# Layer 1's query and key rows by seven Strassen block products, with the weight sums made as layer 1 begins

## The chip, the cores and the metric

The kernel runs on one core of one Trainium2 chip, as one launch. The metric is the device time of one execution in microseconds (us). Below, PE is TensorE, ACT is ScalarE, DVE is VectorE, POOL is GpSimd, and SP is the engine whose queue issues most of the DMAs. b is a batch (0 to 7). KB are KB per partition.

## The reference

Two layers work on x of 8 batches, 512 channels and 1024 tokens, all in FP32. Layer 0 is group norm, eight-head attention over all tokens, a projection and a residual. Layer 1, cut to what matters here:

```python
importance = sum over channels of x*x               # one number per token
idx = top_k(importance, 256)                        # the selected tokens of a batch
q_sel, k_sel, v_sel = (Wq x)[idx], (Wk x)[idx], (Wv x)[idx]
q_sel, k_sel = layer_norm(q_sel), layer_norm(k_sel)
attended = softmax(clip(q_sel k_sel^T * scale)) v_sel
out = Wv x, with the selected tokens' rows replaced by attended
return x + Wo out
```

The changed product is that of the 256 selected tokens (512 channels each) with Wq and Wk side by side: a 256 x 512 matrix times a 512 x 1024 matrix, once per batch.

## The kernel before, in words

**Order.** Layer 0 and layer 1 each lie in a region in which every engine issues its instructions in the order in which the code emits them (L721 and L1518). Between the two regions the scheduler may merge an engine's instructions, so layer 1's first ones can run in the tail of layer 0 where what they need is free. Layer 1's order is written out by hand in two lists, `BATCH` (L63 on) and `END`. A word is a step, its number the part, and each `-` or `+` puts the batch one back or one ahead. `layer1` (L700) walks `BATCH` once per batch t from -1 to 5, and then `END` for the last two batches and what is left of batch 5. In a turn t, `row3` is batch t, `selt0-` batch t-1 and `back2--` batch t-2. Batch 0's rows, counts and values are made in layer 0, so the first turn that does full work is t = 1: batch 1's rows and values beside batch 0's selection.

**A batch in layer 1.** PE transposes eight blocks of 128 tokens (`row`, L277); ACT squares them with a sum (`square`) and keeps them for a DMA out (`keep`, `put`). `spread` and `imp` lay the importance out as a row, and DVE counts for each token how many rank before it (`count`, L317: two compares with a sum and one masked by the lower triangle `before`). `place`, `pick`, `holder` and `who` turn counts into indices; POOL gathers the selected rows (`getx`), PE turns them (`selt`) and ACT keeps them (`selk`, the tile `selT`). `qk` (L516) makes the four blocks of 128 rows: q and k, each of two row blocks, each by four matmuls of 128x512 into one PSUM bank. `stats`, `root` and `norm` (L525 to L549) are the layer norm on those banks, DVE but for the square root on ACT; `normt`, `scale` and `score` make the scores, `clip` to `probk` the softmax, `att`, `attk` and `attput` the attended rows. POOL fetches them back into the values (`fetch`), PE turns the values (`back`), DVE adds the residual (`add`), and SP stores. The values themselves, for the tokens in blocks i and i+4, are seven Strassen products in the steps `va` to `vf` (L404) on sums of token blocks that POOL makes (`xs`, L387, eight adds of 128x128) and sums of weights that POOL makes once (`combine_vo`, L369, four of 128x512, into the tile tvo).

**Memory.** The pools of layer 0 that are released before layer 1 lie one behind the other, by the sizes of their tiles: w0 (8.6 KB), mix (3 KB), op0 with the attention outputs o (24 KB), ep with the 14 score buffers e (56 KB), and then mp0, ap, rp0 and sp. Layer 0's last steps use free e buffers for the last residual tiles (xr_last) and the first counts. Layer 1's pools start at the same byte: rp (12.3 KB), up with two value tiles V (32 KB), mp (47 KB) and op with the residual tiles y (six of 2 KB). All tiles of a pool wait for every user of the released pools on whose bytes the pool lies. tvo and the token sums lie elsewhere, in a pool that both layers share.

**The turn from layer 0 to layer 1.** Layer 0's `finish` (L1506) runs the last output projections (PE L899) and adds their residual on DVE (L1127); each xr_last goes out by an SP DMA (L1130). PE's first instruction of layer 1 waits for the last of those DVE adds.

Of the kernel before, what the change touches and what calls it, by code (L numbers as in the profile page):

```python
# [11 lines left out]
F32 = mybir.dt.float32  # L12
# [53 lines left out]
back6--- row3 square1 xs1 back4--- keep2 square3 back7--- va1 inv-- put2 va0 keep3 put4 row0  # L66
keep1 add6--- ka1 add7--- ka0 put1 put3 att0-- xs0 vb1 vb0 kb0 vc0 row6 square0 kb1 add4---
square6 holder- vd0 who- add3--- kc0 keep6 row7 keep0 row5 square5 kg0 vd1 att1-- keep5 square7
getx- keep7 ve0 finite kf1 kc1 attk1-- kf0 va2 attk0-- xs2 attput-- fetch7-- kd0 fetch4--
spread0 imp0 vc1 fetch3-- ka2 spread1 va3 selt0- imp1 selk0- count1 fetch6-- count7 selt1-  # L70
selk1- fetch2-- vb2 kg1 vf1 fetch5-- vput1- count4 kf2 qk1- ke1 count0 ve1 qk0- qk2- xs3 ka3
put0 stats1- vb3 kd1 root1- back5-- norm1- stats0- kb2 put7 vput2- vput4- fetch1-- count3 vput5-
add5-- stats2- root0- qk3- norm0- vd2 vput7- vput0- stats3- root2- kc2 fetch0-- back1-- kb3
root3- vf0 normt0- vput6- ke0 norm2- vd3 back2-- back0-- normt1- vput3- put5 add1-- scale0-
scale1- vc2 vf2 norm3- normt2- count6 ke2 getv- vc3 normt3- add2-- kc3 kg2 add0-- scale2- kg3
scale3- score0- count2 score1- put6 row4+ square4+ ve3 clip- row1+ row2+ keep4+ ve2 exp0- kd3
vf3 kd2 kf3 probt- count5 place back3-- pick1 square2+ pick0 ke3 probk-
"""
END = """
square1- inv--- row7- keep2- back6---- put4- row6- put2- keep1- square7- xs3- row3- row0-  # L80
att1--- put1- keep7- put7- square3- holder-- add3---- row5- attk1--- va3- keep3- square5- row0
keep5- square0- who-- square6- put5- back7---- back4---- vput2-- add7---- finite- add6----
att0--- keep6- spread0- spread1- getx-- add4---- ka3- imp0- row7 keep0- row1 selt0-- imp1- row4
selk0-- square7 selt1-- kf3- put3- put0- selk1-- keep7 count4- count3- vput7-- square4 square1
put7 keep4 xs2- qk0-- count0- attk0--- stats0-- qk1-- count6- va2- stats1-- keep1 attput---
put6- fetch5--- count5- ka2- root1-- kf2- square0 norm1-- keep0 vput4-- qk2-- vb3- vb2- put1
fetch1--- stats2-- put0 row2 kb2- row6 count2- put4 root2-- square2 vd2- square6 row3 kb3- qk3--
fetch7--- square3 keep2 fetch2--- norm2-- fetch6--- count1- kc2- vf2- root0-- vc2- norm0-- row5
vput6-- ke2- square5 kg2- keep3 normt0-- vd3- keep5 kc3- stats3-- root3-- vput1-- vc3- count7-
va0- ve2- scale0-- fetch0--- vput5-- fetch4--- finite norm3-- normt1-- fetch3--- spread1 kd2-  # L90
ka0- put5 imp1 normt3-- normt2-- xs0- scale3-- spread0 kg3- place- pick1- vf3- scale1-- va1-
keep6 pick0- imp0 back7--- holder- scale2-- score1-- score0-- count5 vb0- back6--- who- ve3-
count3 clip-- kb0- vd0- back0--- ka1- getx- back3--- ke3- vput3-- add6--- kf0- vput0-- xs1- vb1-
add7--- back2--- add3--- kc0- put6 selt0- vf0- vc0- exp0-- add2--- kd3- count6 inv-- selt1-
selk0- vput3- count4 selk1- qk1- probt-- probk-- put2 count7 qk2- kg0- getv-- att0-- attk0--
count1 count2 count0 kb1- place att1-- put3 pick1 ve0- vd1- ke0- pick0 attk1-- stats1- qk0- kd0-
holder vc1- stats0- attput-- who back1--- back5--- kc1- kg1- vf1- root1- ve1- ke1- getx add1---
qk3- vput4- stats2- kd1- va2 kf1- add5--- vput0- norm1- selt0 root0- vput6- fetch2-- norm0-
selk0 back4--- add4--- selt1 ka2 selk1 vput5- normt0- stats3- fetch4-- fetch3-- root2- norm2-
qk2 vput1- stats2 normt1- qk0 root3- kf2 vput2- fetch1-- fetch0-- norm3- qk1 va3 root2 xs3  # L100
scale1- xs2 scale0- normt3- norm2 stats1 stats0 scale3- root1 normt2- scale2- ka3 qk3 vb2 kb2
score0- add0--- vput7- root0 score1- stats3 norm0 root3 vd2 norm3 getv- back4-- clip- exp0-
normt2 back0-- scale2 norm1 vb3 vsel1 inv- probt- add4-- kf3 normt0 add0-- normt3 probk- normt1
fetch7-- scale1 scale3 att0- attk0- kc2 back6-- vselk1 att1- vc2 kg2 vc3 fetch5-- scale0 attk1-
fetch6-- attput- score0 fetch2- kb3 add6-- vd3 fetch1- fetch0- va1 score1 fetch4- clip vsel0
back3-- back5-- ka1 vselk0 fetch6- kc3 kg3 exp0 ve2 fetch5- xs0 back1-- vf2 fetch7- add3-- probt
add1-- fetch3- va0 kd2 ke2 back2-- probk ka0 inv att0 att1 attk0 ve3 attk1 back7-- vb0 xs1 kb0
vb1 add5-- add2-- attput kb1 kf1 vc0 vd0 fetch2 back4- vd1 add7-- kc0 kc1 kf0 vf0 kg0 vc1 add4-
fetch6 kd3 ve0 back6- fetch3 kg1 ve1 kd0 ke0 back3- back1- add6- fetch4 fetch0 kd1 fetch1 vf1
vf3 ke1 fetch5 back5- back2- back7- back0- back4 add3- back6 add1- add2- add5- back2 add0- back0  # L110
ke3 fetch7 add7- add4 add6 back5 add2 back1 back7 add0 back3 add5 add7 add3 add1
# [35 lines left out]
def attention_then_topk_attention(  # L147
# [61 lines left out]
    before = const.tile([P, P], F32, tag="before", name="before")  # L209
# [107 lines left out]
    def count(b, j):  # L317

        cnt = get("r1", ("count", b), [P, 3, NB], "count", 2)
        imps = tiles["imp", b]  # L320
        mine = tiles["col", b][:, j : j + 1]
        lo, hi = j * P, (j + 1) * P
        junk = tiles.get("junk")
        if junk is None:
            junk = pools["rp"].tile([P, N], F32, tag="junk", name=f"junk_{b}_{j}", bufs=1)
        if lo:
            nc.vector.tensor_scalar(
                junk[:, :lo], imps[:, :lo], mine, None, ALU.is_ge, ALU.add,
                accum_out=cnt[:, 0, j : j + 1],
            )  # L330
        else:
            nc.vector.memset(cnt[:, 0, 0:1], 0.0)
        nc.vector.tensor_scalar(
            junk[:, lo:], imps[:, lo:], mine, None, ALU.is_gt, ALU.add,
            accum_out=cnt[:, 1, j : j + 1],
        )
        nc.vector.scalar_tensor_tensor(
            junk[:, lo:hi], imps[:, lo:hi], mine, before, ALU.is_equal, ALU.mult,
            accum_out=cnt[:, 2, j : j + 1],
        )  # L340
# [28 lines left out]
    def combine_vo():  # L369
        b11, b12, b21, b22 = (  # L370
            w["vo"][:, 2 * k : 2 * k + 2, part] for k in range(2) for part in (LEFT, RIGHT)
        )
        t = vp.tile([P, NB, 2 * P], F32, tag="v", name="tvo").rearrange(
            "p (n k) c -> p n k c", k=2
        )
        t1, t2, t3, t4 = (t[:, i] for i in range(4))
        for out_, x_, op_, y_ in (
            (t3, b22, ALU.subtract, b12), (t2, t3, ALU.add, b11),
            (t4, b21, ALU.subtract, t2), (t1, b12, ALU.subtract, b11),
        ):  # L380
            nc.gpsimd.tensor_tensor(out_, x_, y_, op_)
        w["products"] = {1: b11, 2: b21, 3: b22, 4: t4, 5: t1, 6: t2, 7: t3}
# [21 lines left out]
    def value_product(n, bank_, first, at=0):  # L404
        def step(b, i):
            out_ = bank((bank_, b, i))[:, at : at + SPAN]
            for k in range(2):
                if n in (1, 2, 4):
                    left = token_block(b, k + 2 * (n != 1), i + NB // 2 * (n == 4))
                else:  # L410
                    left = tiles["xs", b, i][:, {5: 0, 6: 1, 7: 2, 3: 3}[n], k]
                nc.tensor.matmul(  # L412
                    out_, left, w["products"][n][:, k], start=(first and k == 0),
                    stop=(k == 1), skip_group_check=True,
                )
# [100 lines left out]
    def qk(b, i):  # L516
        which, rb = divmod(i, RT)
        pp = bank(("pp", b, i))
        for k in range(CT):
            nc.tensor.matmul(  # L520
                pp, tiles["selT", b][:, k, ts(rb, P)], w["qk"[which]][:, k, :],
                start=(k == 0), stop=(k == CT - 1),
            )

    def stats(b, i):  # L525
        bs = pools["mp"].tile([P, 6], F32, tag="bs", name=f"lbs_{b}_{i}", bufs=4)
        nc.vector.bn_stats(bs, tiles["pp", b, i])
# [11 lines left out]
    def normal(b, i):  # L539
# [8 lines left out]
        rows_ = get("mp", ("rows", b, which), [P, RT, C], "rows", 2)  # L548
        nc.vector.tensor_scalar(  # L549
            rows_[:, rb, :], tiles["pp", b, i], tiles["mv", b, i][:, 0:1], t,  # L550
            ALU.subtract, ALU.mult,
        )
        done("pp", b, i)
# [33 lines left out]
    def clip(b, _):  # L587

        psc = tiles["sc", b].rearrange("p (a n) -> p a n", n=TOP)
        fin = pools["mp"].tile([P, RT, TOP], F32, tag="sfin", name=f"sfin_{b}", bufs=1)  # L590
# [64 lines left out]
    def residual(b, i):  # L655
        ct, hf = divmod(i, NH)
        t = get("op", ("y", b, i), [P, HALF], "y", 6)
# [11 lines left out]
    def add(b, i):  # L669
# [19 lines left out]
        "vsel": vsel, "vselk": vselk, "selt": selt, "selk": selk, "qk": qk, "stats": stats, "root": root,  # L689
# [10 lines left out]
    def layer1():  # L700
        with ExitStack() as st:
# [19 lines left out]
            with tc.manual_schedule(engines=ORDERED):  # L721
                combine_vo()
# [916 lines left out]
```

## Time and profile before

| | us |
|---|---|
| three runs | 2358.97, 2359.34, 2359.86 |
| median | 2359.34 |
| the profiled execution, own time | 2355.33 |
| its span | 2353.0 |
| PE busy | 2317.2 (98%) |
| DVE busy | 1875.6 (80%) |
| ACT busy | 1479.1 (63%) |
| POOL busy | 1432.8 (61%) |

Layer 1 fills the span from 1909.87 us, PE's first instruction of it, to the end. A row of the view by stretches gives the stretch, its length, the busy time of PE, PE's weight loads, DVE, ACT and POOL with their instruction counts, the granted PE clock (1.00 is full), the DMA share and GB/s. A row of the timeline gives start, length, engine, line, operation, what it writes and reads, and in brackets the idle time before it with the instruction that ended it. In the chain of waits a row is start, length and what ran. An FP32 matmul of the code is two instructions in the trace, a transpose one.

### The profile page before, as it was taken

What the parts mean: (1) busy time and instruction counts of PE and PEld (TensorE: products, weight loads), DVE (VectorE), ACT (ScalarE), POOL (GpSimd) and SP (SyncE); (2) the same over time, 40 slices, a digit from 0 to 9 for tenths busy, and PEclk for the clock granted to TensorE, in tenths of its full rate; (3) what the DMA queues carried; (4) which work ended last, traced back from release to release, by engine and by line L of the source; (5) the groups of instructions that cost most, each with busy time, mean ns of one, the idle gap of its engine ahead of it and who ended that gap; (6) DMA issues with size and microseconds to landing.
All of it is one profiled execution on the core that took longest, in us unless ns stands there. A gap on an engine that the chain in (4) does not pass through costs nothing.

```text
span 2353.0 us, 36692 instructions
## 1 busy us (share of the span) xinstructions
PE 2317.2 (98%) x13164; PEld 1053.6 (45%) x13164; DVE 1875.6 (80%) x3020; ACT 1479.1 (63%) x2024; POOL 1432.8 (61%) x890
## 2 busy tenths in 40 slices
PE   7999999999999999999999999999999999999998
PEld 3333443344344334433443344334433357777766
DVE  4889988988898888888988898888787456777774
ACT  3678766776777577757776777677666534444632
POOL 2668655866676677657765776676556724444334
PEclk9999999999999999999999999999999999999999
DMA  5112222322231222222322222222323443666655
GB/s 197 48 44 67 75 76 70 102 69 73 79 96 53 82 82 89 59 79 79 91 69 77 89 82 60 84 68 55 102 82 117 139 170 118 224 217 226 225 171 173
DMA packets 201236, 244.41 MB, mean 104 GB/s; under 512 B 41930, under 2 KB 111306, under 8 KB 201056
## 3 DMA queue, kind: packets, MB, share of 16 engines
q1 hardware_dynamic: 175392, 198.51, 26.5%
q10 hardware_dynamic: 18144, 31.48, 3.7%
q0 software_dynamic: 7520, 12.09, 1.9%
q8 instruction: 104, 1.70, 0.3%
q14 instruction: 76, 0.62, 0.1%
HBM read 181.42 MB, written 73.14 MB: 108 GB/s over the span
## 4 chain that ended last, share of the span: by engine, by line
PE 89%; DVE 4%; DMA 2%; ACT 2%; issue 2%; POOL 1%; SPq 0%; ACTq 0%; DVEq 0%; POOLq 0%
PE sc L1278 19%; PE av L1358 17%; PE g L1034 15%; PE g L899 10%; PE g L1076 7%; PE b_px L412 4%; PE b_pp L520 4%; DVE high L1292 2%; PE b_py L412 1%; PE den L1374 1%; PE b_sc L582 1%; PE first L899 1%; PE b_pa L629 1%; DVE e L1339 1%; PE last L899 1%
## 5 line engine op out<-in xcount | busy, mean ns | idle before, releaser
L1347 POOL TENSOR_TENSOR es<-es,e 128x1024 f32<-128x1024 f32 x384 | 911.1, 2373 | 167.7 <-ACT e L1342 149.8
L1339 DVE TENSOR_TENSOR e<-e,ns 128x1024 f32<-128x1024 f32 x512 | 611.3, 1205 | 7.3 <-ACT ns L1335 7.3
L1286 ACT COPY e<-sc 128x1024 f32<-128x1024 f32 x512 | 501.7, 1016 | 170.2 <-DVE high L1292 101.7
L1342 ACT ACTIVATE e<-e 128x1024 f32<-128x1024 f32 x512 | 533.3, 1063 | 91.4 <-DVE e L1339 83.9
L1292 DVE TENSOR_TENSOR high<-sc,high 128x1024 f32<-128x1024 f32 x384 | 469.4, 1222 | 121.3 <-PE sc L1278 95.9
L1278 PE MATMUL sc<-q,k 64*128 64x512 f32 x2048 | 512.3, 617 | 4.1 <-DVE high L1292 2.5
L1358 PE MATMUL av<-e,v 128*64 128x512 f32 x2048 | 489.8, 598 | 0.6 <-ACT e L1342 0.5
L1347 POOL TENSOR_TENSOR es<-e,e 128x1024 f32<-128x1024 f32 x64 | 152.5, 2382 | 435.8 <-ACT e L1342 435.8
L1278 PEld LDWEIGHTS sc<-q,k 64*128 64x128 f32 x2048 | 174.5, 186 | 269.9 <-issue 146.9
L1358 PEld LDWEIGHTS av<-e,v 128*64 128x64 f32 x2048 | 135.8, 137 | 292.5 <-issue 235.2
L1034 PE MATMUL g<-wqkv,mix_qk 128*64 128x512 f32 x960 | 231.0, 602 | 1.3 <-POOL wqkv L944 1.3
L899 PE MATMUL g<-o,wp 128*64 128x512 f32 x912 | 206.8, 596 | 0.0
L1034 PE MATMUL g<-x,mix_qk 128*64 128x512 f32 x720 | 169.8, 593 | 0.2 <-ACT v L1093 0.2
L1034 PEld LDWEIGHTS g<-wqkv,mix_qk 128*64 128x64 f32 x960 | 60.9, 136 | 155.2 <-issue 115.7
L899 PEld LDWEIGHTS g<-o,wp 128*64 128x64 f32 x912 | 63.0, 137 | 135.4 <-issue 132.9
L520 PE MATMUL b_pp<-w,selT 128*128 128x512 f32 x256 | 114.0, 593 | 0.0
L1292 DVE TENSOR_TENSOR high<-sc,e 128x1024 f32<-128x1024 f32 x64 | 77.6, 1213 | 38.0 <-ACT e L1286 37.6
L1034 PEld LDWEIGHTS g<-x,mix_qk 128*64 128x64 f32 x720 | 51.6, 137 | 103.3 <-issue 89.7
L648 POOL DMA_INDIRECT V<-sa,at x64 | 64.6, 1009 | 54.1 <-issue 15.2
L426 ACT COPY V<-b_px 128x256 f32<-128x256 f32 x112 | 39.7, 374 | 88.4 <-PE b_px L412 81.2
L1410 POOL TENSOR_TENSOR o<-o,ri 128x512 f32<-128x512 f32 x64 | 81.8, 1278 | 20.8 <-ACT o L1405 10.5
L1303 DVE STREAM_TRANSPOSE mT<-high 128x512 f32<-128x512 f32 x128 | 90.3, 705 | 1.7
(228 smaller groups left out, 2811.1 us busy)
## 6 DMA issues: line engine op xcount, KB each, us to landing
nb<-negd SPq DMA_DIRECT2D x128, 256.0 KB, 3.7
x<-in_x_dram SPq DMA_DIRECT2D x32, 512.0 KB
ri<-rid SPq DMA_DIRECT2D x128, 128.0 KB, 2.9
sx<-xT ACTq DMA_DIRECT2D x64, 256.0 KB, 2.4
mix_qk<-mixd SPq DMA_DIRECT2D x120, 128.0 KB, 2.5
xr<-in_x_dram SPq DMA_DIRECT2D x58, 256.0 KB, 3.3
x1d<-xr SPq DMA_DIRECT2D x58, 256.0 KB, 2.4
sv<-V ACTq DMA_DIRECT2D x56, 256.0 KB, 2.4
```

The source lines that it names most:

```text
L412: nc.tensor.matmul(out_, left, w["products"][n][:, k], start=(first and k == 0), stop=(k == 1), skip_group_check=True,)
L520: nc.tensor.matmul(pp, tiles["selT", b][:, k, ts(rb, P)], w["qk"[which]][:, k, :], start=(k == 0), stop=(k == CT - 1),)
L899: nc.tensor.matmul(out[r, :], wide_[:, r], moving, start=(k == 0), stop=(k == CT - 1),)
L1034: nc.tensor.matmul(pt[r, :], weights[:, k, r], moving[:, k, :], start=(first and k == 0), stop=(k == 1), skip_group_check=True,)
L1076: nc.tensor.matmul(pt[ts(r, HD), ts(j, P)], tokens[:, k, j * P + r * HD : j * P + r * HD + HD], weights[:, k, :], start=(first and j + k = ...
L1278: nc.tensor.matmul(sc[:, hh, :], ks[p][r, ts(j, P)], qs[p][r, ts(hf, HALF)], start=True, stop=True,)
L1286: nc.scalar.copy(raw[t, j], banks["s", t, j])
L1292: nc.vector.tensor_tensor(high[t], banks["s", t, j], raw[t, 0] if j == 1 else high[t], ALU.max)
L1339: nc.vector.tensor_tensor(raw[t, j], raw[t, j], high[t], ALU.add)
L1342: nc.scalar.activation(raw[t, j], raw[t, j], AF.Exp, scale=QK_SCALE)
L1347: nc.gpsimd.tensor_add(sums[t], raw[t, 0] if j == 1 else sums[t], raw[t, j])
L1358: nc.tensor.matmul(avs[t][HD * hh : HD * hh + HD, :], vs[p // 2][:, j, (p % 2) * P + HD * hh : (p % 2) * P + HD * hh + HD], e[:, hh, :], s ...
```

## The change

1. `qk` is replaced by seven products (steps `qa` to `qg`), each two matmuls of 128x512 per half of the channels: a Strassen form with two row blocks, two halves of the channels, and q and k as the two column blocks. Sums of the selected rows (`qs`) are four POOL adds of 128x256, written into a half of the token-sum tile. Products share three banks: qx gets 1, 6, 7 and 4 one on top of the other, qy 5 and 3, qz 2.
2. Between products a bank's state is taken: `ra`, `rb` and `rc` are ACT copies of 128x512, `rf`, `rg` and `rd` are DVE adds of a bank to the SBUF tile `rows`. `stats` and `norm` read three of the four row blocks from `rows` in SBUF, and one from the bank.
3. The sums of Wq and Wk (`combine_outputs`, four POOL adds of 128x1024, one of them in place) follow those of Wv Wo at the start of layer 1's region. Their tile of 12 KB is the first of the pool up.
4. The mask `before` and the unused output `junk` of the counts are BF16.
5. For room, a temporary of `clip` shares the slot of `sT`, and there are five y tiles, not six. rp is 10.3 KB, up 44 KB, mp 45 KB, and op starts 8 KB further on.
6. `BATCH` and `END` are new lists.

```diff
-    before = const.tile([P, P], F32, tag="before", name="before")
+    before = const.tile([P, P], BF16, tag="before", name="before")
...
+    def combine_outputs(name, blocks, in_place):
+        b11, b12, b21, b22 = blocks
+        if in_place:
+            t = pools["up"].tile([P, 3, 2, C], F32, tag=f"t{name}", name=f"t_{name}")
...
+        t2, t3, t4 = (t[:, i] for i in range(3))
+        t1 = b12 if in_place else t[:, 3]
         for out_, x_, op_, y_ in (
             (t3, b22, ALU.subtract, b12), (t2, t3, ALU.add, b11),
             (t4, b21, ALU.subtract, t2), (t1, b12, ALU.subtract, b11),
         ):
             nc.gpsimd.tensor_tensor(out_, x_, y_, op_)
+        w[name, "products"] = {1: b11, 2: b21, 3: b22, 4: t4, 5: t1, 6: t2, 7: t3}
+
+    def combine_weights1():
+        combine_outputs("vo", [
+            w["vo"][:, 2 * k : 2 * k + 2, part] for k in range(2) for part in (LEFT, RIGHT)
+        ], False)
+        combine_outputs("qk", [
+            w[name][:, 2 * k : 2 * k + 2, :] for k in range(2) for name in "qk"
+        ], True)
...
-    def qk(b, i):
+    def selected_sums(b, _):
+        t = tiles["ss", b] = tiles["xs"][:, int(b != B - 2)]
+        a11, a12, a21, a22 = (
+            tiles["selT", b][:, 2 * q : 2 * q + 2, ts(rb, P)] for rb in range(RT) for q in range(2)
+        )
+        s1, s2, s3, s4 = (t[:, n] for n in range(4))
...
+    def selected_product(n, bank_, first):
+        def step(b, _):
+            out_ = bank((bank_, b))
+            for k in range(2):
+                if n in (1, 2, 4):
+                    left = tiles["selT", b][:, k + 2 * (n != 1), ts(int(n == 4), P)]
+                else:
+                    left = tiles["ss", b][:, {5: 0, 6: 1, 7: 2, 3: 3}[n], k]
+                nc.tensor.matmul(
+                    out_, left, w["qk", "products"][n][:, k], start=(first and k == 0),
+                    stop=(k == 1), skip_group_check=True,
+                )
...
+    def selected_take(which, rb, add_of=None):
+        def step(b, _):
+            out_ = rows_of(b, which)[:, rb, :]
+            if add_of is None:
+                nc.scalar.copy(out_, bank(("qx", b)))
+            else:
+                nc.vector.tensor_tensor(out_, bank((add_of, b)), out_, ALU.add)
...
+        "qs": selected_sums, "qa": selected_product(1, "qx", True),
+        "qb": selected_product(6, "qx", False), "qc": selected_product(5, "qy", True),
+        "qd": selected_product(7, "qx", False), "qe": selected_product(3, "qy", False),
+        "qf": selected_product(4, "qx", False), "qg": selected_product(2, "qz", True),
+        "ra": selected_take(0, 0), "rb": selected_take(1, 0), "rc": selected_take(1, 1),
+        "rd": selected_take(1, 0, "qy"), "rf": selected_take(0, 0, "qz"),
+        "rg": selected_take(1, 1, "qy"), "stats": stats, "root": root,
...
-                combine_vo()
+                combine_weights1()
```

The new `BATCH`, whole, in which the prediction follows steps:

```
put4 row3 square1 square3 va0 inv-- keep2 back7--- back4--- keep1 keep3 put1 put3 add7---
back6--- xs0 add3--- put2 att1-- att0-- va1 ka0 vb0 attk0-- kb0 attk1-- row5 attput-- holder-
ka1 row7 vd0 square5 xs1 row0 add6--- who- kc0 square0 row6 kf1 vc0 getx- square7 kg0 square6
keep7 vb1 keep0 keep5 ve0 put0 xs2 finite vput6- spread0 kb1 imp0 spread1 add4--- vc1 kf0 vd1
va2 row4+ imp1 kc1 keep6 count7 selt0- fetch4-- kg1 selk0- count5 fetch3-- ve1 vput2- fetch1--
ka2 square4+ selt1- fetch2-- count3 selk1- fetch6-- qa- qs- keep4+ qg- vput5- ra- vput1-
fetch0-- vput0- va3 qb- rb- kd1 vb2 fetch5-- qd- vput4- kb2 rf- stats0- ka3 root0- count2
fetch7-- count6 rc- qc- kd0 kf3 rg- qf- put5 norm0- stats1- stats3- qe- back2-- vf0 back5-- xs3
root1- vd2 rd- kc2 put7 back1-- put6 vf1 add2-- stats2- vc3 vf2 norm1- add1-- root3- root2-
normt0- ke0 normt1- ke1 vb3 back0-- vput3- norm3- scale1- norm2- add0-- count0 scale0- vc2
normt2- normt3- vput7- kb3 getv- scale2- kg2 scale3- vd3 ke2 kc3 score0- score1- row2+ count1
add5-- ve2 kg3 clip- back3-- row1+ vf3 kd2 kf2 ve3 exp0- kd3 count4 probt- place pick0 square2+
probk- ke3 pick1
```

In the old list the token sums `xs1` stood fourth, and `xs0` behind `att0--`; `vb1` and `vb0` were the first steps to read them.

## The prediction

> **What bounds the kernel now.** I read the page's first part (PE busy for 98% of the span), then the view by stretches for layer 1, then the chain of waits, then the timelines of the turn between the layers. Two stretches in the middle of layer 1:
>
> ```profile
> 2000.00:2050.00 50.00, 49.83 (x265) 38.88 (x264) 35.39 (x112) 26.54 (x64) 23.32 (x40) 1.00 0.69 231
> 2050.00:2100.00 50.00, 49.84 (x268) 39.12 (x267) 33.13 (x103) 24.68 (x62) 20.73 (x36) 1.00 0.69 230
> ```
>
> PE is busy for 49.8 of 50 us; DVE, next, for 33 to 35. The chain runs through PE, and its `qk` rows return at a fixed distance:
>
> ```profile
> 2042.79 3.43 PE b_pp L520 x8
> 2047.08 6.87 PE b_pp L520 x16
> ...
> 2099.55 3.43 PE b_pp L520 x8
> ```
>
> The first and last rows are `qk1-` of two batches: 56.76 us a batch. Eight instructions take 3.43 us, so one 512-column instruction is 0.429 us of PE's time. The other steps by the same chain: a value product of 256 columns 0.86, `va` 1.73, a turn of one block 0.44. PE's work in the old list, so summed, is 56.4 us a batch; only some 0.4 us of a batch is waiting. So in layer 1 the time is PE's work, plus what PE waits at its beginning and end.
>
> **What PE saves.** Before, 16 matmuls or 32 instructions a batch; after, 7 products of 2 matmuls, 28 instructions. Four fewer, 4 x 0.429 = 1.72 us a batch, eight batches: **-13.7 us**. As PE is full from turn 1 to the last `back`, all of it is on the path if the rest keeps up.
>
> **What the products add on other engines, per batch.** ACT: three copies of 128x512, 0.59 us each (the row of `keep`): 1.8 us on 25 busy in 50. DVE: three adds of 128x512 from PSUM, 0.68 each (the row of `add`): 2.0. Off again: three `norm` passes that no longer read PSUM, 0.81 each before; a 128x1024 pass in SBUF takes 0.81 too (the one norm pass of layer 0 on DVE), so at most half, 1.2 us. DVE gains 1 us on some 39 in a batch. POOL: four adds of 128x256, between 0.46 (128x128) and 1.28 (128x512), say 0.75: 3 us on 25. None becomes the bound; I cost them at nothing, with PE as cover. The BF16 mask and `junk`: rows 0.36 (masked) and 1.28 us (1024 wide), all FP32; between no change and halved, on DVE, which is not on the path: nothing, at most 7 us a batch less on DVE. Fewer y slots and the shared slot of `clip`: the next user comes many microseconds later (`clip` 44 us behind the `att` that frees `sT` in the new `BATCH`): nothing.
>
> **New waits between the products.** A product may not add to a bank before the former state is taken. In the new list qb stands two steps of PE (`qg` 1.72, `va3` 1.73) behind qa, for a copy of 0.59. Between qb and qd there is only `vb2`, 0.86, for `rb`, 0.59: 0.27 spare. Between qd and qf there is `qc`, 1.72, for `rc`, 0.59, but `rc` queues on ACT behind `root0`, with a table load 1.28 and 0.2. `root0` waits for `rf` (0.68) and `stats0` (0.70 + 0.18 + 0.15) on DVE, which may start when qg ends, 6.0 us before qd's end (`va3`, qb, `vb2`, qd). Needed before qf: 0.68 + 1.03 + 1.48 + 0.59 = 3.8 us of a 6.0 + 1.7 = 7.7 us way, so DVE or ACT may be 3.9 us late. `qe` waits for `rg`: 1.72 (qf) for 0.68. POOL's sums stand behind five `fetch` at 1.3 us each, which can begin some 9 us before qb: they fit. Bounds: from -3 (the new lists close the 0.4 us a batch that PE waits now) to +8 us (1 us in each batch). I take **+0.5**.
>
> **The weight sums.** This is the dear part. POOL's own rows for such adds, and its first sums of tokens in layer 1:
>
> ```profile
> 1795.24 7.24 POOL L1347 TENSOR_TENSOR es<-es,e 128x1024 f32<-128x1024 f32 x3
> ...
> 1820.91 1.27 POOL L381 TENSOR_TENSOR tvo<-w 128x512 f32<-128x512 f32 x1 [2.95 <-ACT w L1223]
> 1822.26 1.28 POOL L381 TENSOR_TENSOR tvo<-tvo,w 128x512 f32<-128x512 f32 x1
> ```
>
> ```profile
> 1871.59 0.46 POOL L402 TENSOR_TENSOR xs<-x_q,x_k 128x128 f32<-128x128 f32 x1
> ```
>
> The sums for Wv Wo ran at 1820.9, in a gap of layer 0, because their tile is free then. The first eight token sums followed at 1871.6, 44 us before PE read them. The new four adds have 1024 elements; three such adds take 7.24 us above, so four take 9.6. POOL keeps its order in layer 1's region, so **the token sums of batch 1 come behind them**. And their tile is in the pool up, 10.3 to 54.3 KB from where layer 0's pools begin: on mix, on the attention outputs o (11.6 to 35.6) and on ep (from 35.6). All tiles of a pool wait for every user of those, and ep's last user is the DMA out of xr_last. That such waits are real shows in SP's waits, chain and timeline:
>
> ```profile
> SPq L658 <- DMA x1d<-xr_last: 2.0, 1, 2.0
> ```
>
> ```profile
> 1909.85 2.43 DMA x1d<-xr_last
> ```
>
> ```profile
> 1912.35 1.75 SPq L658 DMA_DIRECT2D y<-x1d  x4
> ```
>
> The y pool touches only the last 0.4 KB of ep, and its first load still waited until that DMA landed, at 1912.28. So the new adds start at 1912.35, not in layer 0's tail. They end at 1912.35 + 9.6 = 1921.95. `xs0` follows: by the row 1871.59 and those behind it, its second and sixth add (the ones that `vb0` reads) end 1.0 and 2.8 us after its start, so at 1924.7. PE before:
>
> ```profile
> 1914.27 1.03 PE L412 MATMUL b_px<-w,x_q 128*128 128x256 f32 x4
> ...
> 1915.57 1.96 PE L412 MATMUL b_px<-tvo,xs 128*128 128x256 f32 x8
> ```
>
> Four `row` and two `va` (1909.87 to 1915.13) come ahead, in the new list too, and then `vb0`. There PE now waits until 1924.7: `vb0` would have ended at 1916.0 and ends at 1925.1, **+9.1 us**. POOL, not PE, sets the end of this stretch; `getx` of batch 0 comes behind `xs1`, at about 1929.1, and lands before PE reaches `selt0` (some 13 us of PE's steps later). PE's own waits of this stretch, 1.1 us for `col` and 0.7 for a value add, go mostly, as the others catch up: **-1.5**.
>
> **The clock.** The trace shows what an idle PE costs afterwards. PE waited 1.89 us for POOL in layer 0's tail:
>
> ```profile
> 1847.16 0.64 PE L1374 MATMUL den<-es,ones 128*32 128x256 f32 x8 [1.89 <-POOL es L1347]
> 1847.72 5.40 PE L345 MATMUL g<-w,x 128*128 128x512 f32 x8
> ```
>
> Eight matmuls that take 3.43 us took 5.40; by stretches of 1 us the granted clock (the third column from the end) was
>
> ```profile
> 1848.00:1849.00 1.00, 1.00 (x3) 0.25 (x3) 1.00 (x2) 0.88 (x3) 0.00 (x0) 0.68 0.50 180
> 1849.00:1850.00 1.00, 1.00 (x3) 0.48 (x2) 1.00 (x2) 1.00 (x2) 0.00 (x0) 0.50 0.28 94
> 1850.00:1851.00 1.00, 1.00 (x3) 0.48 (x2) 1.00 (x2) 0.93 (x1) 0.00 (x0) 0.50 0.02 8
> 1851.00:1852.00 1.00, 1.00 (x2) 0.35 (x2) 1.00 (x2) 0.00 (x0) 0.94 (x1) 0.61 0.07 4
> ```
>
> about 3.4 us at half (1.00 again from 1852), 1.7 us lost. After the 11.5 us without work at the kernel's start it lasted longer:
>
> ```profile
> 13.36 6.39 PE L1147 MATMUL bias_row<-wp,bqkv 128*128 128x512 f32 x8
> ```
>
> 6.39 us for 3.43: 3.0 lost. A wait of 9 us lies between: **+2.4**.
>
> The Trainium skill ("TensorE: Matmul & The Clock Gate", "What's actually happening") speaks against such a gap: it says the clock halves after at least one idle window of about 3.4 us and comes back after at least one busy one. The wait of 1.89 us above was already enough, so the measured rows decide; by the page alone the loss would be 1.7 us or more.
>
> **Sum.** -13.7 + 0.5 + 9.1 - 1.5 + 2.4 = -3.2 us. On the profiled execution's 2355.33 that is 2352.1; the median of the runs is 4.0 higher, so 2359.34 - 3.2 = **2356.1**. The end itself I leave as it is: PE's work behind the last `att` (17.8 us before, 18.6 after, by the lists) runs beside eight fetches at 1.3 us, whose landing ends the kernel.
>
> **Rivals.**
> *The weight sums run early* (in layer 0's tail, as the old ones did). For it: POOL is busy for only 33 of 50 us at 1800 to 1850. Against it: the place of the tile. The wait, the clock and the credit go: -13.7 + 0.5 = -13.2, but 9.6 us more on POOL ahead of the sums es that PE already waited 1.89 us for costs 0 to 4. About 2347.
> *The bank hand-over becomes PE's wait* (slower than before). Place: `rc` behind `root0`, each batch. It decides once DVE or ACT are more than 3.9 us late there; two counts (1.85 us each: 1024 elements in two compares and a mask) run just ahead. Each microsecond beyond costs eight. At 1.2 us: 2356.1 - 0.5 + 9.6 = 2365. Against it: DVE idles 15 of 50 us.
> *The lists also close old waits* or PE finds the clock sooner: -3.5 - 0.7 on the sum, about 2352.
>
> **How the numbers follow.** Chances: my sum 0.68 (by its bounds 2353 to 2360), early sums 0.15, hand-over 0.10, better lists 0.07. Within 0.2% (about what a measurement of this kernel can tell from no change) is 2354.6 to 2364.1. Faster: early sums 0.15, better lists 0.06, a quarter of my sum 0.17: 0.38. Slower: 0.08 of the hand-over and 0.02 of mine: 0.10. Same: 0.52. Range 2347 to 2361.5: it leaves out half of the early sums, nearly all of the hand-over and 0.03 of my sum, below 2 in 10.
>
> **What would show it.** Right: the first POOL adds of 128x1024 in layer 1 start at about 1912 and end near 1922; PE idle some 9 us from 1915, released by POOL's token sums; granted clock 0.5 for 3 to 6 us behind it; 28 instructions of 128x512 a batch, and batches 55.0 us apart. Wrong: those adds before 1900; or PE waits for ACT or DVE ahead of qb, qd, qf or qe; or batches over 56 us apart.

## The result, and the profile after

The changed kernel is slower: 2361.86 us in the median of 22 runs (2358.97 to 2365.89), and 2356.31 for the kernel before in the same rounds (22 runs, 2353.84 to 2360.07). The ratio is 1.0026, 95% interval 1.0020 to 1.0032. In a second set of rounds it was 1.0011 (1.0002 to 1.0020). I had forecast 0.9986. The changed kernel's median came out the same both times (2361.86 and 2361.36 us); that of the kernel before lay between 2354.6 and 2360.0 on five occasions, so where a few microseconds matter I lean below on the traces, each of which is one execution.

The span is 2359.8 us (own time 2361.53). Layer 0 ended 1.9 us earlier than in the trace of before, which is not the change's doing: in four of the fourteen traces, that of before among them, PE runs at half clock for 3.4 us behind its wait of 1.9 us at 1847, and their layer 1 begins at 1909.7 to 1910.4; in the ten others it begins at 1907.1 to 1908.5. From PE's first row of layer 1 to the end it is **451.8 us against 443.1**; I had predicted -3.2, and it is +8.7. First the middle, a stretch of 50 us:

```profile
2050.00:2100.00 50.00, 49.84 (x257) 38.01 (x256) 36.15 (x109) 24.59 (x62) 25.03 (x44) 1.00 0.69 232
```

PE is as full as before. DVE is busy for 40.6 us a batch over three whole batches, and for 39.6 before: the 1 us more that I had put down. The chain of waits gives the distance of the batches, by the first product of two batches, one batch apart:

```profile
2048.03 1.72 PE b_qx L550 x4
...
2103.11 1.72 PE b_qx L550 x4
```

55.08 us; from the first to the fourth such row 55.0 on average, and 56.76 before. That is the saving as predicted. The loss is at both ends of layer 1. The view of PE's waits in layer 1:

```profile
PE b_px L424 <- POOL xs L414: 11.5, 2, 10.9
PE b_pt L282 <- ACT xT L292: 2.7, 1, 2.7
...
PE b_py L424 <- DVE V L442: 1.5, 1, 1.5
```

The columns are the total, the number of waits and the longest. The first row was predicted at 9.1, the other two were not. The timelines of POOL and PE show the first:

```profile
1913.88 2.34 POOL L385 TENSOR_TENSOR t_qk<-w 128x1024 f32<-128x1024 f32 x1 [24.48 <-DMA sx<-xT]
...
1923.31 0.45 POOL L414 TENSOR_TENSOR xs<-x_q,x_k 128x128 f32<-128x128 f32 x1
1923.84 0.45 POOL L414 TENSOR_TENSOR xs<-xs,x_q 128x128 f32<-128x128 f32 x1
```

```profile
1924.35 1.22 PE L424 MATMUL b_px<-t_vo,xs 128*128 128x256 f32 x2 [10.93 <-POOL xs L414]
...
1942.61 1.88 PE L550 MATMUL b_qz<-w,selT 128*128 128x512 f32 x4
```

The clock behind the wait, by a stretch of 5 us (the granted clock is the third column from the end):

```profile
1925.00:1930.00 5.00, 4.45 (x30) 3.45 (x29) 0.79 (x3) 1.33 (x4) 4.76 (x13) 0.50 0.00 0
```

Four adds of 2.34 us, then batch 1's token sums, and PE idle for 10.93 us until the second of these was done, as predicted; but the first add starts 5.9 us after PE's first row (1907.99), where I had 2.5 (the releaser in brackets is only the last one before it; the last experiment shows what it waited for). The second loss is at the beginning of `END`, where PE transposes the last rows of batch 6:

```profile
2198.83 0.60 ACT L286 ACTIVATE xT<-b_pt 128x512 f32<-128x512 f32 x1 [2.95 <-DMA sx<-xT]
```

```profile
2201.06 1.11 PE L282 MATMUL b_pt<-ident,x 128*128 128x128 f32 x4 [2.71 <-ACT xT L292]
```

Here ACT's square waits 2.95 us for a buffer xT whose write out has not landed, PE waits for ACT's copies (L292), and after it runs at half clock. By stretches of 2 us:

```profile
2202.00:2204.00 2.00, 1.58 (x8) 1.21 (x7) 1.04 (x4) 1.35 (x4) 0.00 (x0) 0.50 0.02 8
...
2208.00:2210.00 2.00, 2.00 (x17) 1.92 (x16) 1.93 (x7) 1.83 (x5) 0.00 (x0) 1.00 0.68 222
```

Before, the waits at this place were 0.91 and 0.55 us, and the clock stayed full.

### The profile page after: what moved, and what is told of

The parts are those of the page before. It is cut to its first block, busy times and chain, and to the rows that moved or that the text cites. A ratio compares the mean times of both kernels' runs of the same rounds, so it can differ in the third digit from the quotient of the medians.

```text
span 2359.8 us, 36747 instructions
## 1 busy us (share of the span) xinstructions
PE 2310.0 (98%) x13132; PEld 1049.7 (44%) x13132; DVE 1885.1 (80%) x3044; ACT 1488.1 (63%) x2048; POOL 1465.4 (62%) x926
## 4 chain that ended last, share of the span: by engine, by line
PE 90%; DVE 4%; ACT 2%; POOL 1%; DMA 1%; issue 1%; ACTq 0%; SPq 0%; DVEq 0%; POOLq 0%
PE sc L1334 19%; PE av L1414 17%; PE g L1090 15%; PE g L955 10%; PE g L1132 7%; PE b_px L424 5%; PE b_qx L550 2%; PE b_py L424 2%; DVE high L1348 2%; PE den L1430 1%; PE b_sc L631 1%; PE b_pa L678 1%; PE b_qy L550 1%; PE first L955 1%; PE last L955 1%
## 5 line engine op out<-in xcount | busy, mean ns | idle before, releaser
L1360 DVE TENSOR_REDUCE quarter<-mT 128x16 f32<-128x512 f32 x128 | 87.8, 686 | 4.4
L1391 ACT COPY ns<-nb 128x512 f32<-128x512 f32 x128 | 75.1, 587 | 20.1 <-DMA nb<-negd 18.0
```

## The experiments

"Layer 1" is the time from PE's first row of layer 1 to the end of the span. The ratio is to the kernel before in the same rounds.

| run | median, us | ratio, 95% interval | layer 1, us |
|---|---|---|---|
| before | 2354.6 to 2360.0 | | 443.1 |
| changed | 2361.86 | 1.0026, 1.0020 to 1.0032 | 451.8 |
| a0_after_again | 2361.36 | 1.0011, 1.0002 to 1.0020 | 455.0 |
| e1_tokens_first | 2350.07 | 0.9961, 0.9947 to 0.9974 | 439.2 |
| e1_again | 2350.53 | 0.9978, 0.9969 to 0.9988 | 441.8 |
| e2_no_load7 | 2358.73 | 0.9996, 0.9987 to 1.0005 | 447.5 |
| e3_load7_later | 2365.64 | 1.0022, 1.0013 to 1.0031 | 455.7 |
| e4_no_weight_sums | 2349.03 | 0.9956, 0.9942 to 0.9970 | 437.6 |
| e5_tokens_end | 2350.42 | 0.9963, 0.9951 to 0.9975 | 438.1 |
| e6_tokens_no_load7 | 2346.60 | 0.9947, 0.9934 to 0.9961 | 438.0 |
| e7_before_bf16 | 2357.32 | 0.9999, 0.9989 to 1.0009 | 444.5 |
| e8_rows_later | 2347.55 | 0.9967, 0.9954 to 0.9980 | 437.1 |
| e9_rows_kg | 2346.55 | 0.9962, 0.9950 to 0.9974 | 437.2 |
| e10_op_back | 2358.40 | 1.0016, 1.0007 to 1.0025 | 448.6 |

My theory at this point had two parts. *Start*: the weight sums cost time because batch 1's token sums stand behind them on POOL. *End*: in the new `END` PE runs into the rows of batch 6 while batch 7's load holds up the writes of xT. The rivals: PE would meet the same lateness elsewhere; ACT is late because of the softmax and the load does not matter.

**The start: token sums first.**

```diff
-        ], False)
+        ], False); [token_sums(1, i) for i in range(2)]
         combine_outputs("qk", [
...
-                    if name == "load":
-                        load_x1(b)
+                    if name == "load" or (name, b) == ("xs", 1) and i < 2:
+                        name == "load" and load_x1(b)
                         continue
```

> The changed kernel with one move: POOL's token sums of batch 1 (xs0, xs1) are emitted ahead of the sums of Wq and Wk, not behind them. Start theory: the weight sums cost time only because the token sums stand behind them in POOL's order. Then the token sums run near 1871 us as in the kernel before, the 10.9 us wait at vb0 and the half clock behind it vanish, the weight sums hide between 1914 and 1923 us, and the time falls by 9 to 11 us against the changed kernel (near 2351, below the kernel before). Rival: PE only meets the same lateness elsewhere, because getx of batch 0 and then the first product need POOL and the new sums; then the fall is below 4 us and PE waits at selt0 or qa of batch 0.

PE's and POOL's timelines of this run:

```profile
1914.64 1.13 PE L424 MATMUL b_px<-t_vo,xs 128*128 128x256 f32 x4 [1.39 <-ACT V L438]
...
1930.34 1.88 PE L550 MATMUL b_qz<-w,selT 128*128 128x512 f32 x4
```

```profile
1912.09 2.42 POOL L385 TENSOR_TENSOR t_qk<-w 128x1024 f32<-128x1024 f32 x1 [23.00 <-DMA sx<-xT]
```

The wait at `vb0` is 1.39 us and has another releaser (ACT's value copy), the clock stays full, and the weight sums lie hidden from 1912.09 to 1921.7. From the first row to the first `qg` (the only product in the bank qz), a stretch with the same work in both kernels, it is 22.5 us in place of 34.6: 12.1 off, more than expected. Other traces bear it out: 22.3 to 24.1 us in the six with the token sums first, 34.2 to 34.8 in the four with them behind and the pools as in the changed kernel. The result is below the kernel before.

**The whole price of the weight sums.**

```diff
-        t2, t3, t4 = (t[:, i] for i in range(3))
+        t2, t3, t4 = (b12, b22, b21) if in_place else (t[:, i] for i in range(3))
...
-        for out_, x_, op_, y_ in (
+        for out_, x_, op_, y_ in () if in_place else (
```

> The changed kernel without POOL's sums of Wq and Wk: the seven products multiply by the raw weight blocks, so q and k are other numbers; their number, sizes and order stay. It gives the whole price of the weight sums. Start theory: 9 to 11 us off, as in the run with the token sums first, within 1 us of it. Rival: that run keeps part of the price (late getx or late product), so this one is 2 us or more faster than it. If the fall here is below 5 us, the start is not where the time went.

The same stretch takes 21.6 us: 13.0 off the changed kernel. 10 to 12 of the 13 were the order, not the adds (22.3 to 24.1 us with the token sums first); the median is 1.0 us below that of the run with the token sums first, which these runs cannot tell from no difference.

**The end: batch 7's load.** Left out:

```diff
     def load_x1(b):
-
+        if b == B - 1: x1[b] = x1[b - 2]; return
```

> The changed kernel without the 2 MB load of batch 7's input: batch 7 reuses batch 5's tiles, so batch 7's output is that of other data; all other work stays. Load theory: at the beginning of END the writes of xT wait behind this load in full DMA queues, so ACT's squares and then PE's rows wait (2.7 us at 2201) and the clock falls to half (2.8 us more); without the load both go, 4 to 6 us off, near 2357. Rival: ACT is late there because it waits for DVE's row maximum ahead of the exponential (3.8 us at 2186) and the rows stand close together in END; then the load does not matter, less than 1.5 us off, and the wait at 2201 stays over 2 us.

PE's timeline at the beginning of `END`:

```profile
2198.19 1.98 PE L678 MATMUL b_pa<-vs,sT 128*128 128x512 f32 x4 [0.21 <-ACT xT L292]
...
2202.69 1.06 PE L310 MATMUL b_pi<-ident,col 128*128 128x128 f32 x8 [1.01 <-DVE col L304]
```

PE waits 1.2 us in place of 3.1 and the clock stays full: between `qg` of batch 4 and that of batch 5 it is 55.8 us, not 60.7. The time fell by 3.1 us against the changed kernel's median, less than expected; by the ratios to the kernel before (0.9996, against 1.0026 and 1.0011) it is 3.5 to 7 us. So the load matters. Delayed:

```diff
-            steps.append(("load", B - 1, 0))
             steps += [(name, B - 1 + ahead, i) for name, ahead, i in in_order(END)]
+            steps.insert(steps.index(("add", 3, 3)) + 1, ("load", B - 1, 0))
...
-inv--- row6- row5 square6- keep6- ...
+inv--- row6- square6- keep6- ...
-att0--- row0 getx-- ...
+att0--- row5 row0 getx-- ...
```

> The changed kernel with batch 7's load emitted behind the store of the third late add (issued near 2196 us and not 2187 to 2190), and its first row block (row5 of batch 7) two steps later, beside row0. Load theory: xT's writes land some 3 us sooner, PE's wait at 2201 shrinks below 1 us and its clock stays full: 3 to 5.5 us off, near 2357. Rival (ACT held by the softmax): within 1.5 us of the changed kernel, or slower if the rows of batch 7 then wait for the load.

PE's timeline at the same place:

```profile
2200.49 1.06 PE L310 MATMUL b_pi<-ident,col 128*128 128x128 f32 x8 [2.57 <-DVE col L304]
...
2205.57 0.33 PE L282 MATMUL b_pt<-ident,x_k 128*128 128x128 f32 x1 [1.95 <-DMA x_k<-x1d]
```

The wait at the bank is gone, but PE now waits 2.57 us for the column of importances and 3.4 us, in two pieces, for the load itself. That is the ending the rival named, though not its cause. A later load is no remedy (1.0022, between the changed kernel's two ratios).

**The changed kernel again, and BF16 alone in the kernel before.** For the first there is no edit; the second has only the two BF16 lines of the change.

> The changed kernel once more, on the same chip as the three runs beside it, so that they are compared with it and not across chips. By its first runs 1.002 to 1.0032 of the kernel before. The time of layer 1 from PE's first instruction to the end was 451.8 us in its trace and 443.1 in that of before; the same 8 to 9 us between them again if the loss lies in layer 1, and not in the 2 us by which layer 0 differs from one execution to the next.

Layer 1 is 455.0 us, 11.9 above before: the loss lies in layer 1, and its size differs by some 3 us between two executions of one kernel (441.8 and 439.2 with the token sums first). Part of that is the clock: at the beginning of `END` it is at half for 10.2 us in this trace, and for 6.8 in the first one.

> The kernel before with one part of the change alone: the mask and the unused output of the counts in BF16. In the trace of the changed kernel the compare of 896 columns took 1.15 us as before (1.14) and the masked one 0.35: so no change, a ratio within 0.9985 to 1.0015. Rival: DVE's compares become faster with the narrower output, DVE is 5 to 7 us a batch less busy, and the waits of PE for values and columns (1.8 us in all) go: 1 to 2 us faster.

The first part of its page:

```profile
PE 2316.3 (98%) x13164; PEld 1052.3 (45%) x13164; DVE 1875.2 (80%) x3020; ACT 1479.5 (63%) x2024; POOL 1434.4 (61%) x890
```

DVE was busy 1875.6 us before. The mask and `junk` in BF16 change nothing.

**Work ahead of the last row: a miss.** With the token sums first:

```diff
-row0- va3- square3- square5- back7---- keep5- holder-- att1--- back6---- keep3- who-- square0-
-inv--- row6- row5 square6- keep6- ...
+row0- va3- va2- square3- square5- back7---- keep5- holder-- att1--- att0--- keep3- who-- back6----
+square0- inv--- row6- square6- keep6- ...
...
-att0--- row0 getx-- ...
+row5 row0 getx-- ...
...
-va2- count6- selk0-- ...
+count6- selk0-- ...
```

> The run with the token sums first, and in END three steps of PE moved: va2 of batch 6 and att0 of batch 4 come ahead of row6 of batch 6, row5 of batch 7 behind it, beside row0. The End theory says that PE there has no work it may do for 2.5 + 1.4 us while ACT's squares wait for xT, and then runs at half clock; with 3.4 us of work put ahead the waits shrink below 1 us together and the clock stays full: 3 to 5 us faster than with the token sums first alone. Rival: the rows and their column of importances end no sooner, everything behind them is late by the same, and PE waits a little later for the counts or the gather; then less than 1 us.

PE's timeline, the two longest waits, and the chain of waits:

```profile
2188.99 1.98 PE L678 MATMUL b_pa<-vs,sT 128*128 128x512 f32 x4 [2.19 <-ACT xT L292]
...
2193.24 1.09 PE L310 MATMUL b_pi<-ident,col 128*128 128x128 f32 x8 [1.40 <-ACT xT L292]
```

```profile
2179.05 7.92 DMA sx<-xT
```

No gain against the median with the token sums first, as the rival had it: the work that was put ahead needs a PSUM bank too, and the banks are held by rows that ACT could not keep yet. The clock stayed full, but PE waited 4.5 us in five pieces. In this trace an xT write of 256 KB landed 7.9 us after its issue. So I formed another theory: the **row chain**. There are four buffers xT; with writes that land 6 to 8 us after their issue a row gets through each 1.5 to 2 us, whatever PE does, and PE must not enter the rows ahead of its other work. Without the load, on the same chip:

> The run with the token sums first, without batch 7's load (batch 7 reuses batch 5's tiles, so its output is that of other data). Load theory: the waits of 2.5 and 1.4 us shrink to about 1.2 us and the clock stays full, as in the run without the load and with the late token sums: 3.5 to 5 us off against the token sums first. It is the floor for what a better beginning of END can give. Rival: below 1.5 us.

The median is 3.8 us below that of the run with the work ahead, and 3.5 and 3.9 below the two with the token sums first alone. In the trace the longest xT write took 4.4 us and the clock stayed full, yet waits of 1.27 and 2.17 us remain: a shorter chain, not none. I had expected 1.2 us of waits there. From `qg` of batch 4 to that of batch 5 it is 57.9 us, 60.3 and 60.4 with the token sums first and 59.9 with the work ahead. Layer 1 as a whole is no shorter in this trace than in that with the work ahead (438.0 and 438.1).

**Rows later.** With the token sums first, `END` begins so:

```diff
-xs2- put4- row7- row3- keep2- square7- keep7- put2- put7- square1- keep1- row5- add3---- put1-
-row0- va3- square3- square5- back7---- keep5- holder-- att1--- back6---- keep3- who-- square0-
-inv--- row6- row5 square6- keep6- finite- add6----
+xs2- put4- row7- row3- keep2- square7- keep7- put2- put7- square1- keep1- add3---- put1- va3-
+square3- back7---- inv--- keep3- holder-- who-- att1--- va2- row5- square5- keep5- row0- square0-
+row6- square6- keep6- back6---- att0--- finite- add6----
```

> The run with the token sums first once more, on the chip of the two runs beside it: again 0.995 to 0.9975 of the kernel before, layer 1 from PE's first instruction to the end in 438 to 440 us, PE waiting some 4 us for xT's buffers and the column of importances at the beginning of END.

> Token sums first, and the beginning of END in another order: after row7 and row3 of batch 6 PE does va3, back7, holder, att1 and va2, and only then row5, row0 and row6; att0 stands between row6 and the spread, row5 of batch 7 behind it. Row-chain theory: four xT buffers whose writes land 6 to 8 us after their issue let through a row each 2 us or so, and PE had been sent into the rows before its other work; with that work ahead PE waits 1 us or less in place of 4, without half clock: 3 to 4.5 us faster than the token sums first alone (about 435 us for layer 1). Rival: the rows are only later, the counts and the gather of batch 6 with them, and PE waits for these: within 1 us.

PE's timeline:

```profile
2188.37 0.65 PE L282 MATMUL b_pt<-ident,x 128*128 128x128 f32 x4 [0.18 <-ACT xT L292]
```

The wait at the bank is 0.18 us, none is left for the column, the clock is full there; the median is 3.0 us below the token sums first on the same chip (2347.55 and 2350.53), and `qg` of batch 4 to that of batch 5 takes 57.0 us in place of 60.3. The four xT writes still land 5.4 to 7.1 us after their issue in this trace: the chain is as slow as before, and PE no longer waits for it. The row chain stands. Then, in place of "add2--- ve3- kg0-", "kg0- add2--- ve3-":

> The run with the rows later, and DVE's value add kg0 of batch 6 ahead of the late residual add and of ve3, behind the clip. PE's wait of 1.46 us for that add falls to some 0.8: 0.6 us faster, if what stood in front of it was one residual add; nothing if clip's four passes are what it waits for.

PE's timeline at that add:

```profile
2237.25 1.13 PE L424 MATMUL b_py<-w,xs 128*128 128x256 f32 x4 [0.86 <-DVE V L442]
```

The wait is 0.86 us in place of 1.46, as expected; the median is 1.0 us lower, which these runs cannot tell from 0.6 or from nothing (layer 1 is 437.2 us in the trace, 437.1 without this move). This version, **0.9962 (0.9950 to 0.9974)**, beats both kernels.

**Why the weight sums started late.** In the changed kernel the pool of y lies 8 KB further on and off ep's bytes:

```diff
-            for name, bufs in (("rp", 2), ("up", 1), ("mp", 2), ("op", 3)):
+            for name, bufs in (("rp", 2), ("up", 1), ("op", 3), ("mp", 2)):
```

> The changed kernel with the pool of the residual tiles y opened ahead of the pool mp, so that it lies on ep's bytes again: y's first loads and batch 2's load wait for xr_last's writes, as in the kernel before; every other engine's order is the same. In the changed kernel they go out ahead (1899 to 1908 us), the DMA queues are full, and xr_last's last write, issued at 1907.97, holds POOL's weight sums until 1913.88; in the kernel before such a write landed 2.43 us after its issue. Theory: the first weight sum starts 2.5 to 3 us after PE's first row of layer 1 instead of 5.9, PE's wait at vb0 falls from 10.9 to about 7.5 us, and the time by 3 us or a little more, to about 2358. Rival: the sum waits for something else (the first write of xT, as the releaser's name in the trace says): start and wait as in the changed kernel, no gain.

First SP in the changed kernel, then SP's and POOL's rows and PE's wait in this run:

```profile
1904.21 0.93 SPq L245 DMA_DIRECT2D x<-x1d  x2
1907.97 0.32 SPq L1186 DMA_DIRECT2D x1d<-xr_last  x1
```

```profile
1900.09 7.87 SPq L1186 DMA_DIRECT2D x1d<-xr_last  x3
1910.11 1.86 SPq L707 DMA_DIRECT2D y<-x1d  x4
```

```profile
1910.18 2.42 POOL L385 TENSOR_TENSOR t_qk<-w 128x1024 f32<-128x1024 f32 x1 [21.91 <-DMA x1d<-xr_last]
```

```profile
1920.73 1.22 PE L424 MATMUL b_px<-t_vo,xs 128*128 128x256 f32 x2 [7.65 <-POOL xs L414]
```

With y and batch 2's load behind xr_last again, the last write of xr_last takes 2.39 us (the chain of waits has it from 1907.64), the first add starts 2.5 us after PE's first row, and PE waits 7.65 us, not 10.93. From the first row to the first `qg` it is 31.4 us, against 34.2 to 34.8 in the four traces with y further on. The median (2358.40) is 3.0 to 3.5 us below the changed kernel's two, but on another chip; by the ratios, 1.0016 against 1.0026 and 1.0011, the runs do not tell the kernels apart, so the gain rests on the traces. They settle the releaser as well: in the ten traces with y further on and the weight sums in place, the last signal of xr_last's last write comes 3.9 to 5.7 us after its issue (5.7 in the changed kernel's), and the first add starts 0.25 us behind that signal every time. So the place of y, for which my sum had no term, let some 2.5 MB of loads go ahead of the write that the weight sums waited for. The Trainium skill ("DMA: Bandwidth & Descriptors", "Issuing engines are not separate DMA queues") says that transfers started by different engines run on the same 16 DMA engines and interleave; the beginning of `END` agrees, where ACT starts the writes of xT and SP the load of batch 7: those writes land after 5.3 to 7.9 us beside the load, and after 2.1 to 4.4 in the two runs without it.

## Why the prediction was wrong

*PE saves 1.72 us a batch.* Right: 56.76 to 55.0.

*New waits +0.5, nothing for ACT, DVE and POOL.* Right: the copies took 0.58, the adds 0.69, the `norm` pass in SBUF 0.56 and POOL's sums 0.73 us each, and PE waited 0.3 us from 1985 to 2185. The hand-over of the banks never became the bound.

*The weight sums wait for xr_last, and the token sums behind them.* The mechanism was right, and its size was off: +9.1 - 1.5 + 2.4 = 10.0 predicted, 13.0 measured (e4). The wait was 11.5 us with its second piece, not 9.1, because the write that the weight sums wait for took 5.7 us and not 2.43: with a write of 2.39 us PE waits 8.2 us in two pieces (e10). The half clock cost about 3.0 us (PE back at work from 1924.35, full clock again at 1930.8, half of that but for a wait of 0.55), not 2.4. Half clock came behind the long wait in all five traces that have one (7.7 to 10.9 us); but the short wait of 1.89 us at 1847, which I took to be enough, was followed by none in ten of the fourteen traces. PE's old waits of 1.8 us went, as I had it.

*"The end itself I leave as it is"*: **this is the step that failed**. I looked only at the tail behind the last `att` and gave `END` the full credit of three batches, 5.2 us, without following its new order of rows against the four xT buffers and batch 7's load; its loss stood in the sum at nothing, without a reason. From its first row to the end of the span `END` took 168.5 us, and 164.0 before, with 5.2 us less work: 9.7 us lost. Some 4.7 of them are the row chain and the half clock behind it (in the first 16 us PE's time is some 6.5 us above the full-clock durations of its instructions, some 1.8 before; e2 gives 4.9 for the load, e8 against e1_again 3.3 for the order, by the same stretch). 1.5 is one value add that stands behind `clip` on DVE (e9 gets 0.6 back). 1.4 is DVE's adds and the stores behind PE's last `back` (7.7 us, 6.3 before), which was not tried. The remaining 2 us lie in pieces below half a microsecond, and their cause stays open.

Together, with the first two terms as predicted: -13.7 + 0.5 + 13.0 + 9.7 = 9.5, and 8.7 by the traces. Of the cases I named none was this one: the 3.0 us more at the beginning and the 9.7 at the end, much of both set by when a DMA lands, turned the small gain of my sum into a loss.

## What to carry to other kernels

A change that shortens the steady state is priced at its ends: follow every buffer that comes free by a DMA through the first and last turns, and take the landing time from a row in which the queues are as full as they will be there. Work made once goes behind what the first turn reads, on the same engine: here the order of two groups of adds was worth 10 to 12 us, most of what the products save in all eight batches. And a pool that moves by a few KB can lose a wait that kept a large load out of a short write's way.

## What the runs showed of the hardware

The length of PE's idle time does not decide alone whether the clock falls. One wait of 1.88 to 1.89 us for POOL, at 1847, stands in all fourteen traces, behind the same work: in four of them half clock followed, and the eight matmuls behind it took 5.40 us; in ten it did not, and they took 3.70 (e7, which has layer 0 as in before, is one of the ten). Waits of 2.31 (the token sums first, second run, at 2193) and 2.71 us (the changed kernel, at 2201) came with half clock; waits of 2.17 (e6, at 2191), 2.19 (e5, at 2189) and 2.57 us (e3, at 2200) did not, within the next 4 us. The stretches at half clock were 3.4 us (before, from 1848.4), 6.8 (the changed kernel, from 2200.4), 10.2 (e10, from 1917.1) and 13.7 (the changed kernel, from 1917.1): one, two, three and four times the same length. The Trainium skill ("TensorE: Matmul & The Clock Gate", "What's actually happening") has a window of about 3.4 us that runs free of the program; the lengths agree, and that the same wait can go either way would follow from it, though no run here shows where the windows lie. Its advice ("Why this matters for your kernels") to avoid gaps of more than some 3 us does not go far enough by these runs: half clock came behind 1.89 and 2.31 us.
